# The spectral part of a ViT-block-plus-AFNO kernel: two halves of the channels against parts of 4, 2 and 2 channel blocks, the last one kept in SBUF between the inverse transforms

## The chip, the core and the metric

The kernel runs on one core of a Trainium2 chip. The metric is the time of one execution in device microseconds. Every tensor is float32.

## The reference

The input `x` is a 48 x 48 picture of tokens with 768 channels. Layer 0 is a transformer block (layer norm, attention with 12 heads and relative positions, projection, layer norm, MLP of 3072). Layer 1 mixes in the frequency domain and is the part that matters here. Cut to its core:

```python
xf = rfft2(x, axes=(1, 2), norm='ortho')          # 48 x 25 frequencies, 768 channels
xf = xf.reshape(B, H, 25, nb=8, bs=96)            # 8 blocks of 96 channels
o1r = relu(mm(xr, w1[0]) - mm(xi, w1[1]) + b1[0])
o1i = relu(mm(xi, w1[0]) + mm(xr, w1[1]) + b1[1])
o2r = softshrink(mm(o1r, w2[0]) - mm(o1i, w2[1]) + b2[0], 0.01)
o2i = softshrink(mm(o1i, w2[0]) + mm(o1r, w2[1]) + b2[1], 0.01)
y = irfft2(o2r + 1j * o2i, s=(48, 48), norm='ortho')
return y + x
```

The eight blocks never mix: each block of 96 channels can go through the whole of layer 1 alone.

## The kernel before

Layer 0 takes the span up to about 2656 us. Its last loop, the MLP, runs in three passes `p` over 768 tokens each; after each pass `rows_forward(p)` does the forward transform along the rows: for each half `k` of the channels (384 of them) and each group `g` of 384 tokens it makes four products `zp` (L1076), copies each into a tile `zt` of its own (L1080; eight buffers) and writes that to the DRAM scratch `z1[k]` (L1085).

The spectral part (L1127 on) treats the channels in two halves of four blocks. A `Unit(half, k0)` holds four of the 25 frequencies `k` (the last unit of a half only one), so a half has seven units and the whole has 14. A unit goes through four stages, each cut into four steps `i`:

- `columns(i)`: forward transform along the columns for one frequency. One matmul for each block into `fp` (L1202), then a copy to `xf`, by VectorE for even `i` and by ScalarE for odd `i` (`balanced_copy`, L77 and L75). The data `zi` comes from `z1` through `load_frequencies` (L945), two frequencies in one transfer.
- `first(i)`: the first complex layer of one block for all four frequencies, as three real matmuls (`lp`, `lp`, `l`, L1221 to L1223); then a copy on ScalarE, `pre` on VectorE (L1229), two ReLUs on ScalarE (L1234) and a negated copy on GpSimd (L1238).
- `second(i)`: the second complex layer for one frequency, eight matmuls into `mp` (L1252), then bias on VectorE (L1256), clamp on VectorE (L1260) and the difference on GpSimd (L1261).
- `back(i)`: inverse transform along the columns for one frequency, one matmul into `yp` (L1271; one PSUM buffer), copy to `y`, and for each pair of frequencies one write to the DRAM scratch `z2` (L1277).

TensorE's order is written out by hand. In round `r`, for `i` in 0 to 3, it does `back` of unit r-3, `second` of unit r-2, `first` of unit r-1 and `columns` of unit r. When all of a half's `z2` is written, the inverse transform along the rows, `rows_back(half, g)`, can begin: for each of six token groups it loads `zo` from `z2` (L1284, 600 KB, three buffers), then makes three steps of two matmuls into `rps` (L1292; two PSUM buffers, shared with `fp`), adds the residual into `yt` on VectorE (L1295; four buffers) and writes 128 rows of the output (L1296). One such step per step of a round is interleaved from round 12 on for the first half; the rest, and all of the second half's 18 steps, stand after the last round:

```python
                    if r > len(units) // 2 + 4:
                        next(first_half, None)
            for _ in first_half:
                pass
            for _ in pieces(ends[1]):
                pass
```

All transfers of this part are issued by SP (SyncE), in one queue, in an order that the build fixes. A transfer whose data or buffer isn't ready holds up those behind it.

Of the kernel before, what the change touches and what calls it, by code (L numbers as in the profile page):

```python
# [9 lines left out]
F32 = mybir.dt.float32  # L10
# [22 lines left out]
CH = C // 2  # L33
KW = HW // 2 + 1
# [10 lines left out]
def block_then_afno(  # L45
# [49 lines left out]
    z2 = [dram.tile([HW * 2 * KW, CH], F32, name=f"z2_{k}") for k in range(2)]  # L95
# [841 lines left out]
    def load_frequencies(half, k0):  # L937

        rows = z1[half].rearrange("(r k) c -> r k c", k=KW)
        tiles = []  # L940
        for k in range(k0, min(k0 + 4, KW), 2):
            n = min(2, KW - k)
            zi = turn.tile([P, C], F32, name="zi", tag="turn")
            zi = zi[: 2 * HW].rearrange("p (k c) -> p k c", c=CH)
            nc.sync.dma_start(out=zi[:, :n], in_=rows[:, k : k + n, :])  # L945
            tiles.append(zi)
        return tiles

    with ExitStack() as mlp:
# [119 lines left out]
        def rows_forward(p):  # L1069

            for k in range(2):
                for g in (2 * p, 2 * p + 1):
                    for a, parts in enumerate(((0,), (1, 2), (3, 4), (5,))):
# [6 lines left out]
                        zt = turn.tile([2 * 2 * KW, CH], F32, name="zt", bufs=8)  # L1080
# [46 lines left out]
    with ExitStack() as sp:  # L1127
        psum = sp.enter_context(tc.tile_pool(name="ps_spec", bufs=2, space=PSUM))
        cst = sp.enter_context(tc.tile_pool(name="spec_const", bufs=1))
        zin = sp.enter_context(tc.tile_pool(name="spec_in", bufs=2))  # L1130
# [25 lines left out]
        icols = view(2 * HW, 2 * HW)  # L1156
# [18 lines left out]
        NBH = NB // 2  # L1175
# [4 lines left out]
        class Unit:  # L1180
# [4 lines left out]
            def __init__(self, half, k0):  # L1185
                self.half, self.k0 = half, k0
                self.nk = min(4, KW - k0)
                self.n = self.nk * HW
                self.zz = []

            def load(self):
                self.zi = first_loads.pop(0) if first_loads else load_frequencies(self.half, self.k0)

            def columns(self, i):
# [6 lines left out]
                for b in range(NBH):  # L1201
# [4 lines left out]
                balanced_copy(i, self.xf[:, :, :, i, :], fp)  # L1206

            def first(self, i):
# [4 lines left out]
                b = NBH * self.half + i  # L1213
# [28 lines left out]
            def second(self, i):  # L1242
# [3 lines left out]
                zz = mid.tile([2 * HW, NBH, BS], F32, name="zz", bufs=10)  # L1246
                self.zz.append(zz)
                blocks_at = NBH * self.half
                mp = psum.tile([2 * HW, NBH, BS], F32, name="mp2", tag="m")
                for e in range(NBH):  # L1250
                    for t in range(2):
                        nc.tensor.matmul(  # L1252
                            mp[:, e], self.o1[:, e, i, 1 - t : 3 - t].rearrange("p t h -> p (t h)"),
                            a2[:, blocks_at + e, t], start=(t == 0), stop=(t == 1),
                        )
                nc.vector.tensor_tensor(zz, mp, d2[:, ds(blocks_at, NBH)], ALU.add)  # L1256

                flat = zz.rearrange("p n o -> p (n o)")
                cl = mid.tile([2 * HW, CH], F32, name="cl", bufs=3)
# [3 lines left out]
            def back(self, i):  # L1263
# [4 lines left out]
                if i % 2 == 0:  # L1268
                    self.y = mid.tile([2 * HW, 2, CH], F32, name="y", bufs=3)
                yp = psum.tile([2 * HW, CH], F32, name="yp", tag="y", bufs=1)  # L1270
                nc.tensor.matmul(  # L1271
                    yp, icols, zz.rearrange("p n o -> p (n o)"), start=True, stop=True
                )
                balanced_copy(i, self.y[:, i % 2, :], yp)
                if i % 2 or i == self.nk - 1:
                    n = i % 2 + 1
                    nc.sync.dma_start(  # L1277
                        out=z2_h[self.half][:, ds(self.k0 + i + 1 - n, n), :], in_=self.y[:, :n]
                    )

        def rows_back(half, g):

            zo = zin.tile([4 * KW, 4, CH], F32, name="zo", bufs=3)
            nc.sync.dma_start(  # L1284
                out=zo, in_=z2[half][ts(g, 16 * KW), :].rearrange("(a p) c -> p a c", a=4)
            )
            yield
            for i in range(3):
                yt = mid.tile([P, CH], F32, name="yt", bufs=4)
                rp = psum.tile([P, CH], F32, name="rps", tag="f")  # L1290
# [4 lines left out]
                nc.vector.tensor_tensor(yt, rp, x1[:, 3 * g + i, ts(half, CH)], ALU.add)  # L1295
                nc.sync.dma_start(out=out[ts(3 * g + i, P), ts(half, CH)], in_=yt)  # L1296
# [152 lines left out]
```

## Time and profile before

| | |
|---|---|
| median of 3 runs | 2926.68 us (2924.24 to 2931.56) |
| time of the profiled execution | 2924.9 us |
| its span | 2922.9 us |
| TensorE busy in it | 2864.6 us (98%) |
| granted TensorE clock | 0.998 |
| first spectral matmul (`fp`) | 2672.12 us |
| end of the last round's stages, only `rps` left | about 2881.3 us |
| last `yt` (start, length) | 2919.61, 0.56 us |

The span runs from the first instruction to the last; the time of the execution is 2.0 us more. All times that follow are measured from the start of the span. A float32 matmul stands in the records as two, so the counts of the profile are twice those of the code. The records of matmuls overlap; what one costs is the distance to the next.

### The profile page before, as it was taken

To read this page: it belongs to the slowest core of one execution; us is meant where nothing else is said; L and a number is where in the kernel's file an instruction comes from. 1 tells how busy PE (TensorE), PEld (TensorE's weight loads), DVE (VectorE), ACT (ScalarE), POOL (GpSimd) and SP (SyncE) were. 2 spreads that over 40 slices of the span, in tenths; PEclk is the share of its full clock that TensorE was granted. 3 is DMA by queue.
4 is the path that set the end of the run, shared out by engine and by line. 5 is a ranking of instruction groups with operands and counts; after the bars stand their busy time and mean duration, and the time that the engine had idled before them with its cause. 6 is when DMAs were issued, how large, how long until landed. Compare 5 with 4: busy or idle time off the path is not lost. (4 is left out here: it accounts for less than half of the span.)

```text
span 2922.9 us, 40961 instructions
## 1 busy us (share of the span) xinstructions
PE 2864.6 (98%) x15659; PEld 1724.2 (59%) x15659; DVE 1791.0 (61%) x2606; ACT 936.3 (32%) x1514; POOL 609.8 (21%) x564
## 2 busy tenths in 40 slices
PE   7999999999999999999999999999999999999998
PEld 4555665555555555555555555555555555556885
DVE  5243237777777777777733666674666566665564
ACT  1011126656666565665500211122011211102331
POOL 2302110000000000000043322343332323222441
PEclk9999999999999999999999999999999999999999
DMA  3423276173462716435252111212121212113235
GB/s 127 148 88 118 92 162 123 30 135 64 82 128 41 144 34 101 109 59 87 56 177 76 43 56 53 65 64 65 57 65 54 77 54 65 54 57 99 79 93 179
DMA packets 202818, 253.03 MB, mean 87 GB/s; under 512 B 21618, under 2 KB 180978, under 8 KB 201078
## 3 DMA queue, kind: packets, MB, share of 16 engines
q1 hardware_dynamic: 202614, 250.32, 33.5%
q8 instruction: 126, 2.06, 0.3%
q14 instruction: 78, 0.64, 0.1%
HBM read 136.40 MB, written 50.14 MB: 64 GB/s over the span
## 5 line engine op out<-in xcount | busy, mean ns | idle before, releaser
L635 DVE TENSOR_TENSOR acc<-acc,main 128x768 f32<-128x768 f32 x576 | 551.9, 958 | 206.4 <-ACT main L569 149.9
L569 ACT ACTIVATE main<-sp 128x768 f32<-128x768 f32 x648 | 520.8, 812 | 138.9 <-PE sp L565 132.2
L565 PE MATMUL sp<-terms,select 64*128 64x384 f32 x1296 | 413.3, 630 | 0.0
L1051 DVE TENSOR_TENSOR main<-o,main 128x384 f32<-128x384 f32 x540 | 299.4, 557 | 40.3 <-PE o L1049 2.1
L989 PE MATMUL h<-shared,w 128*128 128x384 f32 x864 | 296.7, 486 | 0.8 <-issue 0.8
L559 PE MATMUL sp<-shared 64*128 64x384 f32 x1296 | 268.0, 490 | 2.5 <-DVE o L457 2.2
L559 PE MATMUL sp<-qT,kT 64*128 64x384 f32 x1296 | 266.7, 487 | 0.2
L612 POOL TENSOR_TENSOR inverse<-inverse,rden 128x384 f32<-128x384 f32 x36 | 46.3, 1287 | 1010.7 <-DVE rden L609 918.1
L446 PE MATMUL m<-main 128*128 128x384 f32 x756 | 247.0, 488 | 6.4 <-DVE rstd L121 3.0
L989 PEld LDWEIGHTS h<-shared,w 128*128 128x128 f32 x864 | 164.4, 190 | 116.1 <-issue 2.3
L989 PE MATMUL h<-shared,w1s 128*128 128x384 f32 x648 | 226.6, 486 | 0.0
L582 PE MATMUL op<-main,shared 128*64 128x384 f32 x1296 | 221.2, 488 | 0.0
L582 PE MATMUL op<-main,v 128*64 128x384 f32 x1296 | 219.9, 488 | 0.0
L995 ACT ACTIVATE hT<-c,vec 128x384 f32<-128x384 f32 x108 | 66.4, 615 | 466.2 <-DVE c L1001 466.1
L446 PEld LDWEIGHTS m<-main 128*128 128x128 f32 x756 | 142.6, 190 | 108.3 <-issue 8.7
L1001 DVE TENSOR_TENSOR c<-h,u 128x384 f32<-128x384 f32 x108 | 60.2, 557 | 212.3 <-PE h L989 212.3
L1049 PE MATMUL o<-w,hT 128*128 128x384 f32 x432 | 175.0, 487 | 3.0 <-DVE mv L118 2.0
L1049 PE MATMUL o<-w2s,hs 128*128 128x384 f32 x432 | 174.8, 487 | 3.1 <-DVE hs L155 3.1
L565 PEld LDWEIGHTS sp<-terms,select 64*128 64x128 f32 x1296 | 125.8, 187 | 83.9 <-issue 0.5
L989 PEld LDWEIGHTS h<-shared,w1s 128*128 128x128 f32 x648 | 123.1, 190 | 85.9
L154 POOL TENSOR_TENSOR w1s<-w 128x384 f32<-128x384 f32 x36 | 36.4, 1010 | 610.9 <-PE o L1049 289.4
L559 PEld LDWEIGHTS sp<-shared 64*128 64x128 f32 x1296 | 117.9, 187 | 61.3 <-issue 23.1
(158 smaller groups left out, 3896.8 us busy)
## 6 DMA issues: line engine op xcount, KB each, us to landing
w<-in_mlp_w_dram SPq DMA_DIRECT2D x72, 768.0 KB
terms<-col_parts SPq DMA_DIRECT2D x432, 72.0 KB
terms<-row_hi SPq DMA_DIRECT2D x216, 72.0 KB
terms<-row_lo SPq DMA_DIRECT2D x216, 72.0 KB
main<-in_qkv_w_dram SPq DMA_DIRECT2D x36, 384.0 KB
z<-zt SPq DMA_DIRECT2D x48, 150.0 KB
zo<-z SPq DMA_DIRECT2D x12, 600.0 KB
x<-in_x_dram SPq DMA_DIRECT2D x18, 384.0 KB
```

Source lines behind the costliest of these rows:

```text
L446: nc.tensor.matmul(bank, a[:, c, :], b[:, c, :], start=(first and c == 0), stop=(c == 2), skip_group_check=not first,)
L559: nc.tensor.matmul(sp[:, j, :G], kT[at, ts(kt, P)], qT[at, ts(c, G)], start=True, stop=False,)
L565: nc.tensor.matmul(sp[:, j, :G], select[at, a % 2], ready[pr, c][at, a // 2, b], start=False, stop=True,)
L569: nc.scalar.activation(p, sp[:, :, :G], AF.Exp, scale=HD**-0.5)
L582: nc.tensor.matmul(op[ts(j, 64)], v[:, kt0 + i, ts(j, 64)], ps[i][:, j, :], start=(kt0 + i == 0), stop=(kt0 + i == NT - 1),)
L612: nc.gpsimd.tensor_tensor(inverse, inverse, rden, ALU.add)
L635: nc.vector.tensor_tensor(acc, made[0] if kt == 1 else acc, p, ALU.add)
L989: nc.tensor.matmul(bank[i], a[:, c, :], b[:, c, :], start=(start and c == 0), stop=(c == 2), skip_group_check=not start,)
L995: nc.scalar.activation(h[:, i, ts(k, G)], src, AF.Gelu, bias=col(V_B1 + 2 * n + i))
L1001: nc.vector.tensor_tensor(t, src, other, ALU.add)
L1049: nc.tensor.matmul(bank[k], a, b, start=start, stop=True, skip_group_check=not start)
L1051: nc.vector.tensor_tensor(dst, bank[k], dst, ALU.add)
```

## The change

The channels go through the spectral part in three parts, `PARTS = (0, 4), (4, 2), (6, 2)` (first block, number of blocks), instead of two halves of four blocks.

- There are 21 units in place of 14: seven with four blocks and 14 with two. In a unit of two blocks a step of `columns` has two matmuls, a step of `second` four, `back` has one of 192 columns instead of 384, and `first` is empty in steps 2 and 3.
- The row transforms of part 0 are interleaved in rounds 11 to 16, those of part 1 in rounds 19 to 23 (three steps in each round); the two first loads of a part are issued a round or more ahead. After the last round stand one group of part 1 and the six groups of part 2.
- Part 2 has no scratch in DRAM. `back` copies each frequency's result from PSUM to `y` as before, and then one transfer for each frequency, SBUF to SBUF (72 KB), writes it into `z_last`, a tile of 100 partitions, 24 x 192. For this the inverse matrix has a second form with its output rows sorted by pairs, so that the 96 rows of `y` go to four partitions (`k`, `k`+25, `k`+50, `k`+75), 24 runs of 192 numbers each. `rows_back` then reads `z_last` and has no load.
- To make room, `zo` has two buffers instead of three, and shares them with a tile `zt4` of four `zt` in the MLP (two of these in place of eight single ones).

```diff
-    z2 = [dram.tile([HW * 2 * KW, CH], F32, name=f"z2_{k}") for k in range(2)]
+    z2 = [
+        dram.tile([HW * 2 * KW, n * BS], F32, name=f"z2_{k}")
+        for k, (_, n) in enumerate(PARTS[:-1])
+    ]
...
-            zi = zi[: 2 * HW].rearrange("p (k c) -> p k c", c=CH)
-            nc.sync.dma_start(out=zi[:, :n], in_=rows[:, k : k + n, :])
+            zi = zi[: 2 * HW, : 2 * n * BS].rearrange("p (k c) -> p k c", k=2)
+            nc.sync.dma_start(out=zi[:, :nk], in_=rows[:, k : k + nk, ds(c, n * BS)])
...
+                    zt4 = turn.tile([P, 4, CH], F32, name="zt", bufs=2)
...
-                        zt = turn.tile([2 * 2 * KW, CH], F32, name="zt", bufs=8)
+                        zt = zt4[: 2 * 2 * KW, a]
...
+        z_last = zin.tile([4 * KW, HW // 2, PARTS[LAST][1] * BS], F32, name="z_last")
...
                 yp = psum.tile([2 * HW, CH], F32, name="yp", tag="y", bufs=1)
+                yp = yp[:, : self.nb * BS]
                 nc.tensor.matmul(
-                    yp, icols, zz.rearrange("p n o -> p (n o)"), start=True, stop=True
+                    yp, icols[:, int(self.part == LAST)], zz.rearrange("p n o -> p (n o)"),
+                    start=True, stop=True,
                 )
                 balanced_copy(i, self.y[:, i % 2, :], yp)
-                if i % 2 or i == self.nk - 1:
+                if self.part == LAST:
+                    nc.sync.dma_start(
+                        out=z_last[self.k0 + i :: KW], in_=self.y[:, i % 2, :]
+                    )
+                elif i % 2 or i == self.nk - 1:
...
-            zo = zin.tile([4 * KW, 4, CH], F32, name="zo", bufs=3)
-            nc.sync.dma_start(
-                out=zo, in_=z2[half][ts(g, 16 * KW), :].rearrange("(a p) c -> p a c", a=4)
-            )
+            if part == LAST:
+                zo = z_last[:, ts(g, 4)]
+            else:
+                zo = turn.tile([P, 4, CH], F32, name="zo", tag="zt", bufs=2)
+                zo = zo[: 4 * KW, :, : n * BS]
+                nc.sync.dma_start(
+                    out=zo, in_=z2[part][ts(g, 16 * KW), :].rearrange("(a p) c -> p a c", a=4)
+                )
...
+        def in_turn(part):
+            gens = [rows_back(part, g) for g in range(T // G)]
+            for gen in gens[:2]:
+                next(gen)
+            yield
+            for g, gen in enumerate(gens):
+                for _ in range(3):
+                    next(gen)
+                    yield
+                for later in gens[g + 2 : g + 3]:
+                    next(later)
...
-                    if r > len(units) // 2 + 4:
-                        next(first_half, None)
-            for _ in first_half:
-                pass
-            for _ in pieces(ends[1]):
-                pass
+                    for part in range(len(PARTS) - 1):
+                        begin = per * (part + 1) + 3 + part
+                        if (r, i) == (begin, 3) or (begin < r <= begin + 6 and i < 3):
+                            next(ends[part])
+            for part in ends:
+                for _ in part:
+                    pass
```

## The prediction

> **What bounds the kernel now.** I read the page first, then the windows of the spectral part, then what TensorE (PE) waits for in it, then the chain of waits.
>
> ```profile
> PE 2864.6 (98%) x15659; PEld 1724.2 (59%) x15659; DVE 1791.0 (61%) x2606; ACT 936.3 (32%) x1514; POOL 609.8 (21%) x564
> ```
>
> PE bounds the whole; the change can only win where PE stands still after 2672 us. The windows of the spectral part (busy time of PE, weight loads, VectorE, ScalarE, GpSimd, then clock, DMA share, GB/s) are its first rounds, its other rounds and what comes after the last round:
>
> ```profile
> 2672.10:2757.70 85.60, 82.16 (x713) 75.11 (x713) 50.59 (x113) 34.08 (x92) 37.71 (x44) 1.00 0.31 92
> 2757.70:2881.30 123.60, 122.20 (x973) 104.39 (x974) 72.15 (x162) 43.88 (x124) 49.81 (x62) 1.00 0.34 102
> 2881.30:2922.90 41.60, 32.40 (x97) 17.39 (x95) 13.94 (x25) 0.00 (x0) 0.00 (x0) 0.99 0.66 215
> ```
>
> The last window is the place: PE is idle for 9 us of 41.6 and DMA is twice as busy. The waits of PE from 2672 us name the transfers and GpSimd:
>
> ```profile
> PE rps L1292 <- DMA zo<-z: 5.2, 5, 1.6
> PE mp L1252 <- POOL o L1238: 3.7, 10, 0.4
> PE rps L1292 <- DVE yt L1295: 0.7, 1, 0.7
> ```
>
> The chain gives the price of each matmul group and the shape of the end:
>
> ```profile
> 2699.62 0.68 PE fp L1202 x8
> 2700.30 0.65 PE yp L1271 x2
> 2700.95 1.36 PE mp L1252 x16
> 2703.28 0.68 PE fp L1202 x8
> ...
> 2715.58 0.65 PE yp L1271 x2
> ...
> 2881.31 6.17 PE rps L1292 x20
> 2887.49 6.80 DMA zo<-z
> 2894.42 3.87 PE rps L1292 x12
> 2898.29 7.30 DMA zo<-z
> 2905.73 3.87 PE rps L1292 x12
> 2909.60 5.73 DMA zo<-z
> 2915.47 4.12 PE rps L1292 x12
> 2919.61 0.56 DVE yt L1295
> ```
>
> PE's work adds up from these: 50 steps of `columns` at 0.68, 48 of `first` at 3 x 0.33 and 8 narrow ones at 0.47, 50 of `second` at 1.36, 50 of `back` at 0.65, 36 of `rps` at 1.29: 34.0 + 47.0 + 3.8 + 68.0 + 32.5 + 46.4 = 231.7 us. From 2672.1 to 2919.6 there are 247.5 us, so 15.8 us are idle. Of these 7.5 lie after 2881.2 (38.4 us for 24 steps of 1.29 = 30.9). The rest is mostly round boundaries: a round takes 2715.58 - 2700.30 = 15.28 us where four steps of 3.66 make 14.64. The 0.64 is the wait for the last negated block:
>
> ```profile
> 2713.51 0.41 PE L1252 MATMUL mp<-shared,o 96*96 96x96 f32 x2 [0.40 <-POOL o L1238]
> ```
>
> The timeline has ten of these: rounds 2 to 7 and 9 to 12.
>
> **The work that is cut up.** A matmul costs its columns: 0.085 us a record at 96, 0.163 at 192, 0.323 at 384. Halving `yp` and `rps` changes 50 and 72 records by 0.003: +0.2 us. Bounds 0 and +2 (weight loads of 128 columns are not shown behind 192-column matmuls; the nearest, 96 behind 96, fit in 0.085). The MLP's `zt4` lets a copy wait for the transfers of the group before last, instead of the eighth before; a group takes 3.9 us, and the last 192 KB output had moved 1.4 us after its issue, so I take 0 (bounds 0 and 2).
>
> **Gain 1: no `zo` loads for the last 18 steps.** The 7.5 us go, as far as nothing new is late.
>
> **Gain 2: boundaries.** In a unit of two blocks the last `first` stands in step 1, not 3. Its chain (copy 0.32, `pre` 0.55, two ReLUs 0.80, negation 0.70, with gaps some 2.8 us) then has 3.9 us of PE work in front of its reader. Rounds 9 to 12 lose their wait: 4 x 0.64 = 2.6. Rounds 2 to 7 keep it.
>
> **Gain 3: the very end.** The last add shrinks from 0.56 to about 0.35 (the 384-column form takes 0.554, the 96-column one 0.254) and the last write is half as long: 0.4.
>
> Together 10.5 us; no more than that is there to be had.
>
> **Loss 1: one `yp` buffer.** A copy of `yp` ends about 0.8 us after its matmul at 384 columns, 0.65 at 192. Before, `first` or `second` always stood between two `yp`. Now round 8, steps 2 and 3, has only `columns` (0.34) between: two waits of 0.5, and one of 0.3 in round 16. In round 22 VectorE's fixed order puts the bias and clamp of the last unit ahead of the copy of `yp`: 0.65, and again 0.65 in front of the last `yp`. Sum 2.6; bounds 0 and 5.
>
> **Loss 2: SP's queue.** Every transfer of the part stands in one queue, now 25 SBUF writes more and the `z2` writes, outputs and loads of two parts. The queue order of the changed kernel shows three loads close to their use. The load of the last unit's `zi` stands behind the write of unit 16's last frequency, one round step before it is needed; 3.0 us of PE work against a copy, two issues of 0.3 and a 72 KB transfer: 0.2 us. The loads of part 1's groups 4 and 5 (300 KB) stand behind the `z_last` writes of round 22's first and round 23's only `back`. Counting from PE's last step of `back` in round 22, step 0: that copy ends at 1.95, its write is issued at 2.0, the load at 2.35; the lone part of a transfer starts 0.75 after its issue (last output: issued 2920.2, moving from 2921.0). With some 2.4 us for 300 KB it lands at 5.5, where PE arrives at 5.3: 0.25. Group 5's load is issued after the last `y`, at 6.3, lands at about 9.6, and PE has been waiting since 7.6: 2.0. Together 2.5. Bounds: 0, and 7 if 300 KB take as long as 600 KB did (5.7 to 7.3). Behind a waiting `rps` stands everything, since it is PE's own queue.
>
> **Loss 3: the pace of the end.** 24 steps of 192 columns alternate between two PSUM buffers: 0.66 of matmul, `yt` starts 0.27 behind, takes 0.35, and PE goes on 0.1 later: two steps in 1.38, or 0.69 instead of 0.65: 24 x 0.04 = 0.9. If `yt` stayed at 0.56 it would be 0.8 a step, 3.6 in all. `yt` has four buffers, 2.8 us around; an output lands about 1.9 us after its add if nothing stands ahead of it.
>
> **The `z_last` writes.** No row of before shows a transfer into four partitions. The nearest rows: 128 partitions alone (the last output) against 100 partitions alone (a `zo`), with the DMA share next to last:
>
> ```profile
> 2921.00:2921.50 0.50, 0.00 (x0) 0.00 (x0) 0.00 (x0) 0.00 (x0) 0.00 (x0) 1.00 0.94 356
> 2912.25:2912.90 0.65, 0.65 (x4) 0.39 (x3) 0.43 (x1) 0.00 (x0) 0.00 (x0) 1.00 0.60 201
> ```
>
> So the shape decides how many of the 16 engines work. At full share 72 KB take 0.2 us; if one engine in four works, at a sixteenth of 356/0.94 GB/s each, 0.8; if a packet of 768 bytes costs as much as one of 1536 (144 packets in about 0.6 us on 16 engines, 0.065 each) then 24 x 0.065 = 1.6. No row decides; I take the middle, 0.8. With nine writes from round 21 on that is 7 us in the 25 us until `z_last` is read, behind group 5; 1.6 would be 14 and still fit. So 0; bounds 0 and 2.
>
> The Trainium skill, "DMA: Bandwidth & Descriptors", section "Why a DMA increments its semaphore by 16 and not by 1", says that a transfer uses the largest number of engines up to 16 that divides the slowest dimension of both sides: 10 of 16 for 100 partitions, which the 0.60 bears out, and 4 for this write. By it the cost would be the 0.8 to 1.6 taken above and not 0.2; it speaks against the new write, though not enough to turn the sum.
>
> **Sum.** -10.5 + 0.2 + 2.6 + 0.2 + 2.3 + 0.9 = -4.3 us: 2924.9 - 4.3 = 2920.6 for the profiled execution. The median before is 1.8 higher than that execution, so I predict 2926.68 - 4.3 = 2922.4 us, 0.15% less. A measurement of this kernel can tell about 0.3%, or 8.8 us, from no change; so the forecast is no measurable change.
>
> **Rivals.**
> *All of the idle goes.* The loads of groups 4 and 5 come in time and the copies are faster than I reckon: -10.5, 2916.2 us. For it: losses 1 and 2 rest on gaps of tenths. Against it: group 5's load can't be issued before the last `y`. It is over 0.3% by 1.7 us only.
> *The idle moves.* The end, with no loads, runs at the pace of its 24 small outputs and their four buffers: if one takes 3.6 us around instead of 2.8, a step costs 0.9, 24 x 0.21 = 5 more than my sum: +0.7, 2927.4 us. For it: after 2887 us `yt` waited twice for an output (3.5 us). Against it: there 600 KB loads stood ahead.
> *Slower: the writes into four partitions bound the end.* They are 25, from round 17 on; until `z_last` is read PE has about 52 us of work. From 2.3 us each on the engines they share they take the lead, at 2.6 they finish 13 us late: +9, 2935.5 us. For it: their engines also carry `zo`, `zi` and outputs. Against it: 288 KB of `zi` at 3072-byte runs took 2.4 from issue to end.
>
> **How the numbers follow.** Forecast 0.52, all idle gone 0.25, idle moved 0.13, slower 0.10. Faster by over 0.3%: 0.25 and 0.04 from the forecast's better edge, 0.29; within: 0.48 + 0.13 = 0.61; slower: 0.10. The forecast's own range is 2917 to 2928 (the bounds of losses 1 to 3). The range reaches from 2914 (all idle gone, and 2 us of the median's height above the profile gone with the loads) to 2931 (idle moved and loss 2 at its upper bound); the slower rival stays outside.
>
> **What would show it.** Right: in the windows the last 25 us have PE at 95%; `zo` waits only for part 1's last groups, about 2 us; `mp` waits for GpSimd in rounds 2 to 7 only; `rps` of 192 columns 0.69 apart. Wrong: PE waiting for `z_last`'s writes, or for `zi` (`fp`), by more than 1 us; `yt` waiting for outputs; rounds of two blocks longer than 7.4 us without `rps` (then a copy or GpSimd chain has become the bound).

## The result and the profile after

The changed kernel takes 2936.24 us (median of 20 runs, 2928.46 to 2942.47), the kernel before beside it 2928.77 us (20 runs, 2922.69 to 2934.20). The ratio is 1.0028, with a 95% interval of 1.0022 to 1.0035: slower by 0.28%, just inside what the prediction called no measurable change, but 20 runs a side tell it apart from 1. The forecast was 4.3 us less, and the range ended at 2931.

Layer 0 ends some us earlier or later from run to run (the first `fp` starts at 2667.8 to 2677.1 us over all profiles here), so I compare the **spectral part**: from the start of the first `fp` to the end of the span. It took 2922.9 - 2672.1 = 250.8 us before and 2926.7 - 2667.8 = 258.9 us after: +8.1 us, against +7.5 us between the medians. The whole loss is there.

The first line of the page hardly moves, with 2864.6 us before:

```profile
PE 2865.8 (98%) x15781; PEld 1741.6 (60%) x15781; DVE 1803.0 (62%) x2700; ACT 939.7 (32%) x1538; POOL 617.6 (21%) x589
```

The windows of the spectral part (columns as in the prediction; it starts 4.3 us earlier here, so the edges are moved with it, but for the second, which lies 1.0 us further on; the last window of before is cut in two):

```profile
2667.80:2753.40 85.60, 82.16 (x713) 75.11 (x713) 50.40 (x113) 34.02 (x92) 37.69 (x44) 1.00 0.27 81
2753.40:2876.00 122.60, 118.88 (x922) 104.68 (x923) 76.72 (x212) 42.53 (x128) 46.13 (x73) 1.00 0.42 121
2876.00:2901.00 25.00, 21.95 (x175) 20.14 (x173) 14.27 (x45) 6.16 (x20) 8.02 (x14) 1.00 0.37 105
2901.00:2926.70 25.70, 20.04 (x96) 18.42 (x96) 8.59 (x24) 0.00 (x0) 0.00 (x0) 0.85 0.39 124
```

The first rounds are the same to the hundredth. The middle, which had 1.4 us of idle TensorE, now has 3.7; the end is no longer short of DMA (share 0.37 and 0.39 for 0.66), and TensorE still stands for 8.7 us in the last two windows: it is busy for 78% of the last 25.7 us, where the prediction asked for 95%. And the last clock is 0.85. What TensorE waits for in the part:

```profile
PE yp L1285 <- DVE y L78: 3.9, 6, 1.0
PE rps L1317 <- DMA zo<-z: 3.2, 2, 1.7
PE mp L1264 <- POOL o L1251: 2.5, 7, 0.4
PE fp L1213 <- DMA zi<-z: 1.1, 1, 1.1
PE yp L1285 <- ACT y L76: 1.1, 3, 0.5
```

Before, there was no wait on `yp` or `zi` at all. The five `zo` waits have become two, and GpSimd's ten have become seven: those two gains came. How the `yp` wait is made shows in round 18, step 3 (TensorE's line, then VectorE's):

```profile
2864.02 0.54 PE L1285 MATMUL yp<-zz,shared 96*96 96x192 f32 x2 [1.04 <-DVE y L78]
...
2862.68 0.35 DVE L1268 TENSOR_TENSOR zz<-mp,shared 96x192 f32<-96x192 f32 x1 [0.44 <-PE mp L1264]
2863.02 0.35 DVE L78 COPY xf<-fp 96x192 f32<-96x192 f32 x1
2863.29 0.32 DVE L1272 TENSOR_SCALAR cl<-zz 96x192 f32<-96x192 f32 x1
2863.53 0.34 DVE L78 COPY y<-yp 96x192 f32<-96x192 f32 x1
```

The matmul into `yp` of step 2 was issued at 2861.47 and its copy could have run ahead of `zz`; VectorE had stood idle for 0.44 us until 2862.68. In VectorE's program it comes behind `zz`, `xf` and `cl`. The chain of waits has SyncE's issues in it (SPq), which before it did not:

```profile
2874.97 0.35 DVE y L78
2875.34 0.64 SPq L1292
2876.04 0.46 SPq L1322
2876.60 0.64 SPq L1292
2877.34 2.70 DMA zi<-z
2880.08 0.58 PE fp L1213 x4
...
2900.89 0.64 SPq L1292
2901.63 0.63 SPq L1292
2902.36 5.09 DMA zo<-z
2907.59 16.16 PE rps L1317 x84
```

L1292 is the write to `z_last`: 0.64 us to issue, each. And the granted clock (the third column from the end) in the tail:

```profile
2902.00:2905.50 3.50, 3.50 (x11) 3.50 (x12) 0.71 (x2) 0.00 (x0) 0.00 (x0) 0.51 0.52 157
2908.80:2912.20 3.40, 3.40 (x13) 3.30 (x12) 1.09 (x4) 0.00 (x0) 0.00 (x0) 0.51 0.27 87
2912.20:2924.00 11.80, 11.53 (x67) 10.28 (x66) 6.00 (x18) 0.00 (x0) 0.00 (x0) 1.00 0.40 134
```

Twice TensorE runs at half its clock for 3.4 us, after it had waited for a `zo`: eleven and thirteen matmul records there, where the full clock has some 20 (67 in 11.8 us). About 1.7 us are lost each time. The two stretches have the same length, and the last section shows what decides whether a wait brings one.

### The profile page after: what moved, and what is told of

Same layout as the page of the kernel before. It is cut to its first block, busy times and chain, and to the rows that moved or that the text cites. A ratio compares the mean times of both kernels' runs of the same rounds, so it can differ in the third digit from the quotient of the medians.

```text
span 2926.7 us, 41582 instructions
## 1 busy us (share of the span) xinstructions
PE 2865.8 (98%) x15781; PEld 1741.6 (60%) x15781; DVE 1803.0 (62%) x2700; ACT 939.7 (32%) x1538; POOL 617.6 (21%) x589
```

## The experiments

All comparisons are with the kernel before on the same chip. The ratio is of medians over many executions. "Spectral part" is from one profiled execution of each kernel, and how much it varies between executions was not measured. In two runs the profiled execution lay far above its median (`z_last` issued by ScalarE: 2953.3 for 2944.3 us; by pairs with outputs by ScalarE: 2935.3 for 2930.6); there the ratio is the better guide. "At clock 0.50" adds up the stretches of the spectral part in which TensorE had half its clock; of what TensorE runs in them, half is lost.

| kernel | spectral part, us | at clock 0.50, us | ratio of times, 95% interval |
|---|---|---|---|
| before | 250.8 | 0 | 1 |
| changed | 258.9 | 6.8 | 1.0028 (1.0022 to 1.0035) |
| two halves of `yp` | 259.4 | 10.2 | 1.0043 (1.0028 to 1.0059) |
| early `zo` | 254.6 | 0 | 1.0017 (1.0007 to 1.0026) |
| `yp` halves, early `zo` and `zi` | 257.7 | 3.4 | 1.0028 (1.0015 to 1.0041) |
| last part by DRAM | 262.4 | 15.3 | 1.0044 (1.0028 to 1.0059) |
| two parts of four, by DRAM | 261.0 | 6.8 | 1.0042 (1.0026 to 1.0057) |
| wide `y` | 257.5 | 13.7 | 1.0023 (1.0012 to 1.0034) |
| wide `y`, early `zo` and `zi` | 256.6 | 3.4 | 1.0025 (1.0015 to 1.0034) |
| the same with `yt` halves | 250.7 | 3.4 | 0.9993 (0.9983 to 1.0003) |
| `z_last` issued by ScalarE, early loads | 274.6 | 30.7 | 1.0062 (1.0048 to 1.0076) |
| VectorE by hand | 265.1 | 6.8 | 1.0049 (1.0033 to 1.0064) |
| VectorE by hand, all buffers | 258.7 | 0 | 1.0021 (1.0013 to 1.0030) |
| `yt` halves, rows one round later | 252.2 | 3.4 | 0.9997 (0.9987 to 1.0006) |
| `yt` halves, rows two rounds later | 254.1 | 3.4 | 1.0011 (0.9998 to 1.0023) |
| one round later, loads by pairs | 250.8 | 3.4 | 0.9999 (0.9990 to 1.0009) |
| `yt` halves, last outputs by ScalarE | 250.2 | 0 | 1.0005 (0.9996 to 1.0013) |
| by pairs, last outputs by ScalarE | 256.4 | 10.2 | 1.0012 (1.0003 to 1.0020) |

### Taking the change apart

**Last part by DRAM.** The parts stay 4, 2, 2, and the 25 writes to `z_last` become 13 writes to a third `z2` and six loads.

```diff
-        for k, (_, n) in enumerate(PARTS[:-1])
+        for k, (_, n) in enumerate(PARTS)
...
-        LAST = len(PARTS) - 1
-        z_last = zin.tile(...)
+        LAST = -1
```

> Parts of 4, 2 and 2 blocks as in the changed kernel, but the last part goes through a third scratch tensor in DRAM and is read back by eight-group loads like the others; the 25 writes to `z_last` become 13 writes of pairs. Theory A: `yp` waits as they are (6.7 us); zi's 1.2 us gone or halved, as SyncE issues half as many in the last rounds; at the end the groups of the last part are read back by loads of half the width (102 packets-deep, about 150 KB) behind the last column transforms: a wait of 2 to 3 us before the first and 0.5 to 1 us before each later one, so 4 to 8 us; the spectral part takes 259 to 264 us, slower than the changed kernel by 0 to 5 us: the direct way is worth that much. Theory B (the issues and writes of `z_last` cost the time): 253 to 256 us, faster than the changed kernel.

Measured: 262.4 us, within the expectation of theory A, so with the direct way the part is 3.5 us shorter. This is a net figure, and mostly clock: without the direct way TensorE runs for some 13 us at half clock and loses 6.5 us by it, where the changed kernel loses 3.4. Of the rest, the `zo` waits are 4.9 us longer (a load of the last part has 300 KB here, not the 150 of the expectation), and the `yp` and `zi` waits are 4.6 shorter. The waits on `yp` of rounds 18 to 22 all but went (0.9 us left from round 16 on), with the same single `yp` buffer:

```profile
PE rps L1316 <- DMA zo<-z: 8.1, 4, 3.7
PE yp L1284 <- ACT y L76: 0.9, 3, 0.5
```

VectorE's program had another order here: pre, y, zz, xf, cl. So the single buffer alone does not make these waits.

**Two parts of four, by DRAM**, that is, the same with `PARTS = (0, 4), (4, 4)`: the parts of the kernel before with the row transforms, loads and two `zo` buffers of the changed one.

> Two parts of four blocks, both through DRAM, as in the kernel before; of the change there stay the row transforms in turn with loads two groups ahead, the two `zo` buffers in place of three, and the order in which the first part's row transforms stand after the later rounds. Theory A: rounds 9 to 12 lose their waits at the boundary as in the changed kernel (2.6 us less than before), round 8/9's and the halved yp waits of parts of two blocks are absent, and the end reads six groups by loads of 614 KB, two ahead: 7 to 10 us of waits there, as before or 1 to 3 us more with one buffer less; 248 to 252 us. A rival: the row order itself costs what the change cost: 255 us or more.

Measured: 261.0 us, so the rival held. Four things that are longer than before make nearly 9 of the 10.2 us. `rps` waits for `zo` 10.0 us for 5.2, since three row transforms stand between the last `back` and the first load's data where the kernel before kept six in hand (the first of these waits is 5.3 us). Behind that wait the clock is at 0.50 until 2900.16, which costs TensorE some 2.3 us. GpSimd's waits are 13 for 10, or 1.1 us more, and waits on `yp` make 0.7. The three kernels give a path: the row transforms' new order with two `zo` buffers +10.2 us, the cut into 4, 2, 2 another +1.4, the direct way -3.5; together +8.1. Each step has the clock of its profile in it, and the sizes hold in this order only.

### The `yp` waits

**Two halves of `yp`.** One PSUM tile whose two halves of 192 columns alternate.

```diff
...
+                    yp = yp_pair[0][:, ts(i % 2, self.nb * BS)]
```

> In the parts of two blocks the PSUM buffer `yp` becomes two halves of 192 columns that alternate; the part of four blocks keeps its one buffer. Theory A (each new wait has a cause of its own, and the 8.1 us that the spectral part grew, from 250.8 to 258.9 us, are their sum): the waits on `yp` of rounds 16 to 22 (0.5 + 1.2 + 1.0 + 1.0 + 2.0 = 5.7 us) go, round 8/9's 1.0 us stays, the zi and zo waits stay; the spectral part takes 253 to 255 us, the whole some 4 to 5 us less than the changed kernel. Theory B (SyncE's queue paces the last rounds: 25 issues for `z_last` at 0.64 us each, and the loads behind them): the waits on `yp` go, but TensorE then arrives earlier at zi and at the zo loads of groups 4 and 5 and waits there longer; the spectral part stays above 257 us. Theory C (the lost time is VectorE's, which is full in the rounds of two blocks): the waits move to `fp` and `mp2` of the same rounds, and 258 us stay.

Measured: 259.4 us; the `yp` waits add up to the same within 0.1 us. The step that was 1.04 us late:

```profile
2870.70 0.54 PE L1291 MATMUL yp<-zz,shared 96*96 96x192 f32 x2 [1.04 <-DVE y L78]
```

Step 3 still waits for VectorE's copy, which is step 2's, out of the other half. The edit did not give TensorE a second buffer, and so tells nothing of what one would bring. There is no second bank to give it: all eight are in use.

**Wide `y`.** Three SBUF tiles `y` hold twelve results in place of six; nothing of PSUM changes.

```diff
-                if i % 2 == 0:
+                if i % (4 if self.part == LAST else 2) == 0:
                     self.y = mid.tile([2 * HW, 2, CH], F32, name="y", bufs=3)
+                    if self.part == LAST:
+                        self.y = self.y.rearrange("p a (b c) -> p (a b) c", b=2)
...
```

> In the last part one SBUF tile `y` holds four column results of 192 in place of two, so that the same three tiles cover twelve writes to `z_last` in place of six; nothing else is changed. In the changed kernel VectorE's program places the copy out of `yp` of rounds 18 and 19 behind zz, xf and cl of the next step; with this edit it stands ahead of zz again (pre, y, zz, xf, cl). Theory A (the waits on `yp` of rounds 18 and 19 come from VectorE's order, which is arranged around `y` tiles that come free late behind the slow writes to `z_last`): 1.2 + 1.0 + 1.0 us and some of round 22's go; the spectral part falls from 258.9 to 254.5 to 256 us; zi and zo waits and the half clock in the tail stay, or TensorE arrives earlier there and waits up to 1 us more. Theory B (one PSUM buffer of `yp` is too few for steps of two blocks, whatever VectorE's order): the waits stay, 258 to 259 us.

Measured: 257.5 us, where theory A had 254.5 to 256. VectorE at the same step as above:

```profile
2865.93 0.56 DVE L1242 TENSOR_TENSOR pre<-lp,p_both 96x384 f32<-96x384 f32 x1 [0.61 <-ACT p_both L1240]
2866.40 0.34 DVE L78 COPY y<-yp 96x192 f32<-96x192 f32 x1
2866.92 0.35 DVE L1268 TENSOR_TENSOR zz<-mp,shared 96x192 f32<-96x192 f32 x1 [0.18 <-PE mp L1264]
```

The copy is ahead of `zz`, and with it all of VectorE's waits on `yp` in rounds 18 to 22 are gone, 4.5 us: theory A in its cause. Not in its sum: some 3 us of it came back at the next late load.

```profile
2903.23 3.25 PE L1321 MATMUL rps<-zo,shared 100*128 100x192 f32 x9 [3.58 <-DMA zo<-z]
```

```profile
2901.70:2908.40 6.70, 4.21 (x12) 3.70 (x12) 1.07 (x3) 0.00 (x0) 0.00 (x0) 0.50 0.50 150
2908.40:2915.20 6.80, 6.32 (x20) 6.35 (x21) 1.43 (x4) 0.00 (x0) 0.00 (x0) 0.50 0.20 63
```

TensorE came earlier to the same late load, waited 3.6 us for 1.5, and then ran at half clock for 13.7 us. The windows' clock was 1.00 again after that.

**VectorE by hand.** VectorE's order in the last part's rounds as the code is written.

```diff
...
+                if r == 2 * per:
+                    by_hand.enter_context(tc.manual_schedule(engines={mybir.EngineType.DVE}))
```

> The changed kernel, with VectorE's instructions of the last part's rounds in the order in which the kernel is written (y, zz, cl, both, pre, xf, yt step by step, as TensorE's already are) in place of the order that the scheduler finds. No buffer and no load is changed. Theory A: the waits on `yp` of rounds 18 to 22 go (3.2 and some 1.3 of 2.0 us), the waits for zi (1.2 us) and zo (3.4 us, or up to 2 us more as TensorE comes earlier) and the half clock stay: 255.5 to 257.5 us. Theory B (the copies of `y` really wait for the writes to `z_last` that read their tile): the waits on `yp` stay, 258 us or more, and the profile shows VectorE's y waiting for a DMA.

Measured: 265.1 us. VectorE's waits on `yp` went, and no `y` waited for a write to `z_last`, which is against theory B; but the written order has both operands `both` behind `cl`, and `l` waits for them fifteen times, 0.4 to 0.7 us each and 7.8 in all (shown below in the run that has everything else too). It missed the number by 8 us.

### The loads and what stands behind them

**Early `zo`.** Two groups share a `zo` buffer in part 1; a load goes three groups ahead.

```diff
+                    if g % 2 == 0:
+                        zo_pair[:] = [turn.tile([P, 4, CH], F32, name="zo", tag="zt", bufs=2)]
+                    zo = zo_pair[0].rearrange("p a c -> p (a c)")[: 4 * KW, ts(g % 2, 4 * n * BS)]
...
-            for gen in gens[:2]:
+            ahead = 2 if PARTS[part][1] == NBH else 3
...
```

> In part 1 the row transforms' groups share the two `zo` buffers two by two, and a group's load is issued three groups ahead in place of two. Nothing else changes. Theory A: the waits for zo of groups 4 and 5 (1.7 and 1.7 us) go, and with them both stretches at clock 0.50 in the tail (some 3.5 us), if it is the idle TensorE that brings the clock down; the spectral part takes 251.5 to 253 us. Theory B (SyncE's queue): the loads stand behind the same writes to `z_last`, whatever the buffer; less than 1.5 us is won. Theory D (the clock falls in the tail by itself, as nothing but short row transforms run there): the waits go and the half clock stays: 255 to 256 us, and the profile shows a granted clock of 0.50 in the last 25 us.

Measured: 254.6 us, -4.3, between the numbers of theories A and D. No wait for `zo` is left and the granted clock is 1.00 to the end, as A has it and against D. A new wait came: TensorE 1.25 us for `yt`, and VectorE 1.8 us for the output that held the buffer.

```profile
2912.80 4.40 PE L1325 MATMUL rps<-z_last,shared 100*128 100x192 f32 x24 [1.25 <-DVE yt L1329]
...
2912.39 0.36 DVE L1329 TENSOR_TENSOR yt<-rps,main 128x192 f32<-128x192 f32 x1 [1.81 <-DMA out_dram<-yt]
```

**`yp` halves, early `zo` and `zi`**: the two edits above, and the last unit's load one round earlier.

```diff
-                if r < len(units):
+                if r < len(units) - 1:
                     units[r].load()
+                if r == len(units) - 2:
+                    units[r + 1].load()
```

> The two halves of `yp`, the half buffers of `zo` three groups ahead, and the last unit's load of zi one round earlier, all together. Theory A: 5.7 (`yp`) + 1.2 (zi) + 3.4 (zo) + 3.5 (clock) = 13.8 us less at most; 12 us taken, so a spectral part of 245 to 248 us, below the 250.8 of the kernel before, and a ratio to the kernel before of 0.998 to 0.999. Theory B (SyncE's queue paces the last rounds): 3 to 6 us are won and the tail waits for zo or `z_last` take the rest; 253 us or more, ratio 1.000 or above. Theory D (half clock by itself): 249 to 251 us, ratio 0.999 to 1.000, with a granted clock of 0.50 in the tail.

Measured: 257.7 us, three more than with the early `zo` alone and on theory B's side by the number, but not by its waits: none is for `zo` or `z_last`. The wait for `zi` is gone, and VectorE's program has changed with the loads: five of the waits on `yp` in rounds 20 to 22 are new or longer (0.5, 0.9, 0.9, 0.9, 0.9 us).

**Wide `y`, early `zo` and `zi`**: the same with the wide `y` in place of the `yp` halves.

> The wide `y` tile, the half buffers of `zo` with loads three groups ahead, and the last unit's load of zi one round earlier. Theory A (order of VectorE, late zi, late zo, and the half clock as a consequence of the idle): from the 254.6 us with the early zo alone, 3.2 to 4.5 us (`yp`) and 1.2 us (zi) go, which gives 249 to 250.5 us, against 250.8 in the kernel before: a ratio of 0.999 to 1.000. Theory B (SyncE's queue paces the end: the 25 issues at 0.64 us and the outputs behind them): what is won in rounds 18 to 20 comes back as waits of `yt` for its outputs, of the first row transforms of `z_last`, or at half clock; 252 us or more.

Measured: 256.6 us, on theory B's side. From round 18 on, all waits on `yp` but 1.2 us, and those on `zi` and `zo`, are gone, and this stands in their place:

```profile
PE rps L1329 <- DVE yt L1333: 6.6, 7, 1.4
DVE yt L1333 <- DMA out_dram<-yt: 4.9, 5, 1.8
```

But the first five of the seven lie ahead of the tail, where VectorE waits for no output: there `yt` stands behind `zz`, `cl` and `pre` of later steps in its program, as `y` did.

**The same with `yt` halves.** In parts of two blocks a `yt` tile holds two results.

```diff
...
+                    if (3 * g + i) % 2 == 0:
+                        yt_pair[:] = [mid.tile([P, CH], F32, name="yt", bufs=4)]
+                    yt = yt_pair[0][:, ts((3 * g + i) % 2, n * BS)]
```

> The kernel with the wide `y` and the early zo and zi loads, and besides, in the parts of two blocks, a `yt` tile of 384 columns holds the results of two row transforms: eight half buffers in place of four. In the run without this, TensorE waited 6.6 us for `yt` in rounds 20 to 22 and the tail: VectorE's program had `yt` behind the next steps' zz and cl, and in the tail `yt` waited for outputs up to 1.8 us. With it VectorE's program has yt ahead of zz in rounds 20 and 21. Theory A (VectorE's order, arranged around buffers that are taken to come free late, sets where TensorE waits): 4 to 6 us of these go, the spectral part takes 250.5 to 252.5 us. Theory B (SyncE's queue is too slow for the last rounds and the end): the waits for `yt` move on to the tail, 255 us or more.

Measured: 250.7 us, within theory A's 250.5 to 252.5, and 0.9993 in time: the kernel before is reached. 5.9 us came from a buffer, with the same work on every engine.

**VectorE by hand, all buffers**, is this kernel with VectorE's order as written, and nothing else.

> VectorE's order by hand in the last part's rounds, with the wide `y`, the half buffers of `zo` and `yt`, and the early zo and zi loads. Theory A: of the waits only round 8/9's 1.2 us, the last rounds' yp (0.7) and some outputs' stay; the spectral part takes 247.5 to 250.5 us, against 250.8 in the kernel before, and the ratio to it is 0.999 to 1.000. Theory B (SyncE's queue): 253 us or more, with waits of `yt` for outputs or of TensorE for `z_last` in the tail.

Measured: 258.7 us. Between the two only VectorE's order differs, and it moves the spectral part by 8.0 us, as much as the whole change did, and the medians by 6.2. The half clock is no part of it: this run has none, the other 3.4 us.

```profile
PE l L1236 <- DVE both L1231: 6.1, 12, 0.7
```

(The line covers the rounds from 2840 us on; three more of these waits, 1.8 us, lie ahead of it.) Both theories missed: A by its number, and B, whose number of 253 or more was met, by the waits that it named: they are for `l`, and only one, of 1.2 us, stands before `z_last`.

**`z_last` issued by ScalarE**, with the early loads.

```diff
-                    nc.sync.dma_start(
+                    nc.scalar.dma_start(
                         out=z_last[self.k0 + i :: KW], in_=self.y[:, i % 2, :]
```

> As the changed kernel with the early zo and zi loads, and the 25 writes to `z_last` are issued by ScalarE in place of SyncE; `y` stays as it was. It tells what the writes cost SyncE's queue from what their transfers cost. VectorE's order has the copies of `y` ahead of zz here too. Theory A: ScalarE loses some 0.6 us for each of 25 issues, beside its copies of a few us a round; its activation of `o` and copies of p_both come later, and `mp2` waits for `o` 0.3 to 0.6 us in rounds 17 to 21; the outputs no longer wait behind `z_last` on SyncE, so `yt` waits for nothing: 249 to 252 us. Theory B (SyncE's queue is what paces the end): 246 to 248 us, below the kernel before by 3 us or more.

Measured: 274.6 us, far off both. Half of the writes take a `y` that VectorE copies. ScalarE's queue stands until that copy is done, and its own work behind it:

```profile
PE yp L1285 <- ACT y L76: 9.3, 6, 2.4
```

A window there:

```profile
2910.00:2920.00 10.00, 10.00 (x47) 9.74 (x46) 3.08 (x11) 1.15 (x5) 1.66 (x3) 0.50 0.15 47
```

Five stretches at 0.50, 30.7 us together, lie between 2869.7 and 2927.8 us, each behind such a wait (1.9 to 2.4 us), with a clock of 1.00 between them. The issue costs 0.64 us here too, so the price goes with the write, not with SyncE; whether its shape or its target in SBUF makes it was not taken apart. What the writes cost SyncE's queue was not learned from this.

### What ends last, once the waits are gone

With the `yt` halves one wait is left in the tail, before the first row transform of `z_last`. The profile puts it down to an output; the issue of the last two writes to `z_last` ends 3.9 us ahead of its end (timeline, SyncE's line and TensorE's):

```profile
2900.71 1.37 SPq L1296 DMA_DIRECT2D z_last<-y  x2
...
2905.95 14.09 PE L1336 MATMUL rps<-z_last,shared 100*128 100x192 f32 x72 [1.67 <-DMA out_dram<-yt]
```

**Rows one and two rounds later** put nine and twelve row transforms of part 1 in between, for six.

```diff
-                        begin = per * (part + 1) + 3 + part
+                        begin = per * (part + 1) + 3 + 2 * part
```

> The kernel with the wide `y`, the half buffers of `zo` and `yt` and the early loads (spectral part 250.7 us), and besides, part 1's row transforms start one round later, so that nine of them in place of six stand between the last column transform and the first row transform of `z_last`. In the run without this, TensorE stood 1.7 us before that first row transform, which the profile puts down to an output; the last write to `z_last` had left SyncE 3.9 us earlier. Behind the wait the granted clock was 0.50 for some 3.5 us (1.7 us lost). Theory A (the wait is for the last write to `z_last` to land, and the half clock follows from the idle): both go, 247 to 248.5 us, a ratio of 0.998 to 0.999 to the kernel before. Theory B (the wait is for outputs in SyncE's queue, or the clock falls at this place anyway): 249.5 us or more, and a granted clock of 0.50 in the last 20 us.

> The same with part 1's row transforms two rounds later: twelve of them behind the last column transforms, none in rounds 19 and 20. Theory A: what was one wait is covered already with nine, so nothing more is won: within 0.7 us of the run with one round later. If VectorE's yt copies of rounds 19 and 20 held up something there, 0.5 to 1 us less. Theory B (outputs in SyncE's queue pace the end): the three more row transforms come in the stretch that their outputs already fill, so 1 to 2 us more than with one round later.

Measured: 252.2 and 254.1 us. The first row transform of `z_last` waits for nothing in either, as theory A has it; but group 5's load is now late instead (3.0 us, and 3.4), and half clock follows in both. Theory A's numbers missed. Theory B's came (249.5 or more, and one to two more for the second), but by this load and not by the outputs that B names.

**One round later, loads by pairs**: groups 0 to 3 at the start, 4 and 5 behind group 1.

> The kernel with part 1's row transforms one round later (spectral part 252.2 us), and its zo loads issued by pairs: groups 0 to 3 at the start, groups 4 and 5 behind group 1. With one round later alone, the first row transform of `z_last` waited for nothing, but group 5's waited 3.0 us for its load, issued 5 us before, behind the last writes to `z_last`; the clock was 0.50 for 3.4 us behind it (1.7 us). Theory A (a late load is what is left, the half clock its consequence): both go, 247 to 248.5 us, with no granted clock under 0.9 ahead of the end, and a ratio of 0.998 to 0.999 to the kernel before. Theory B (something always ends late in the tail, as the writes to `z_last`, the outputs and the loads share SyncE's queue and the transfers): a wait of 1.5 us or more stands elsewhere, 250 us or more.

Measured: 250.8 us. The load is in time; now `yt` waits 2.2 us for an output and the first `rps` of `z_last` 1.25 us, and half clock follows. Theory B's number.

**Last outputs by ScalarE**, on the kernel with `yt` halves and on the one by pairs.

```diff
-                nc.sync.dma_start(out=out[ts(3 * g + i, P), at], in_=yt)
+                (nc.scalar if at_end else nc.sync).dma_start(out=out[ts(3 * g + i, P), at], in_=yt)
```

> The kernel with the wide `y`, the half buffers of `zo` and `yt` and the early loads (spectral part 250.7 us), and besides, the outputs of the row transforms that stand after the last round are issued by ScalarE, which has nothing else to do there, in place of SyncE. In the run without this TensorE stood 1.7 us before the first row transform of `z_last`, and the clock was 0.50 for some 3.5 us behind it. Theory A (that wait is for the last writes to `z_last` to land, which the outputs in the same queue hold up little): the wait stays within 0.7 us of 1.7, and so does the half clock: 250 to 251 us. Theory B (outputs in SyncE's queue make it late): the wait falls under 0.5 us and the half clock goes: 247 to 248.5 us, a ratio of 0.998 to 0.999.

> The same edit on the kernel whose row transforms come one round later with loads by pairs (250.8 us). There `yt` waited 2.2 us for an output ahead of the first row transform of `z_last`, which so came 1.3 us late, with a half clock behind it. Theory A (the transfers are slow, the queue does not matter): within 1 us of 250.8. Theory B (outputs queue on SyncE behind the writes to `z_last`): the 1.3 + 1.7 us go, 247 to 248.5 us, a ratio of 0.998 to 0.999, below both the kernel before and the changed one.

Measured: 250.2 and 256.4 us. In the first theory A's number came (250 to 251), and the wait did not go, though the outputs had left SyncE's queue. It even grew, to more than A allows, and the half clock that A keeps went. It grew because the last two writes to `z_last` left later, behind an output of the rounds that waited for its `yt`:

```profile
2903.85 1.37 SPq L1296 DMA_DIRECT2D z_last<-y  x2
...
2908.54 12.47 PE L1337 MATMUL rps<-z_last,shared 100*128 100x192 f32 x72 [2.79 <-issue]
```

Its windows, with the clock at 1.00 in spite of that wait:

```profile
2904.00:2908.00 4.00, 1.75 (x11) 1.36 (x9) 1.07 (x3) 0.00 (x0) 0.00 (x0) 1.00 0.47 147
2908.00:2912.00 4.00, 3.46 (x20) 3.24 (x21) 1.43 (x4) 0.00 (x0) 0.00 (x0) 1.00 0.40 129
```

The last issue ends at 2905.22, TensorE goes on 3.3 us later. SyncE's queue holds nothing but these two writes then (the outputs of 2903.42 and before are out, the next is issued at 2908.89). It moves its last ten packets between 2907.5 and 2908.0 and none from there to 2908.6, so the wait is for these writes to land, as theory A has it. In the second, `yt` waits twice for outputs, 3.0 and 2.7 us, more than without the edit, and both numbers missed. Here the last `z_last` writes left SyncE at 2910.1 to 2912.6, behind two outputs of the rounds, some 5.7 us later than without the edit, and TensorE's second wait ends 2.3 us after them. Why the second of those outputs was issued so late is not shown. None of the sixteen kernels beats the one before; five can't be told from it.

## Why the prediction was wrong

**Gain 1 (no `zo` loads for the last 18 steps): right.** No such load is in the tail, and the last 18 row transforms wait for nothing. By the gaps between TensorE's starts it brought 6.8 us.

**Gain 2 (boundaries): right, less.** Three of four waits went, one of 0.4 stayed: 1.7 us for 2.6.

**Loss 1 (one `yp` buffer): the step that failed first.** The places in round 8, 16 and 22 were right, and cost what was said or a little more. Rounds 18 and 19 were missed: 1.2 + 1.0 + 1.0 us. In all 6.7 us for 2.6, above the bound of 5. The term looked for two `yp` with too little work between, and used VectorE's order in round 22 only. In round 18 there is work enough between; the copy itself stands behind `zz`, `xf` and `cl`. Wide `y` and VectorE by hand both change VectorE's order and leave the single `yp` as it is, and in both these waits are gone, so VectorE's order is shown as their cause. Alone, wide `y` won only 1.4 us of the part, since other waits and the clock took the rest. That the scheduler places `y` and `yt` late because it takes their buffers to come free late, behind the writes to `z_last`, fits all of these runs, but what the scheduler assumes was not seen.

**Loss 2 (SP's queue): the right loads, too short.** `zi` 1.2 us for 0.2, `zo` 3.4 for 2.25. An issue was taken at 0.30 us, and the write to `z_last` takes 0.64; the load of group 5 took 5.1 us from its issue to its landing for the 3.2 of the estimate (0.75 + 2.4), though within the bound of 7. The wait for `zi`, by over 1 us, is one of the signs of being wrong that the prediction named.

**A term that was not there: the clock.** Two stretches at half, some 3.5 us in all. The kernel before has the same kind of waits in its tail (five, up to 1.6 us) at a clock of 1.00, and I took the clock for given. By the last section part of this is luck: it depends on where a wait falls. With these terms (4.1 + 0.9 + 1.0 + 1.2 + 3.5 us, and 0.7 less from gain 1) the sum goes from -4.3 to +7.1 of the 8.1 measured; the remaining 1.0 us is not placed.

**Loss 3 (pace of the end): right.** From 2913.5 to 2923.8 us a step takes 0.69. **Gain 3 (the very end): right.** The last add takes 0.36 us for 0.56, and what follows it 2.54 for 2.73: 0.4.

**The `z_last` writes: the price was near.** One of them moves alone, from 2859.25 to 2860.30 us: 1.05 us for the 0.8 taken, at a DMA share of 0.25 (next to last column), a quarter of the 16 engines:

```profile
2859.50:2860.00 0.50, 0.50 (x8) 0.50 (x7) 0.50 (x2) 0.31 (x1) 0.19 (x1) 1.00 0.25 80
```

**The range** was too narrow at its slow end: the upper bounds of losses 1 to 3, all taken together, give 2932, not 2928. But 2936 lies above that too, so this is not where it failed.

**The rivals.** The slower one came nearest in time, but not by its mechanism: in the changed kernel TensorE never waits for a write to `z_last`. (One of ScalarE's copies into `y` is put down to such a write, 1.8 us at 2899.45, with 0.54 us of waiting on `yp` behind it; with the wide `y` the same 0.5 us are there without it.) The mechanism is real, though, one layer down: of the three kernels that came to 250 or 251 us, two end on that wait (1.7 and 2.8 us). "The idle moves" is what the experiments show at every turn, but by VectorE's order and late loads, not by the outputs' four buffers, which came into play only with the early `zo`.

## What to carry to other kernels

A change that cuts the work finer rearranges every engine whose order is not fixed by hand: price it by the new program order of each, from buffers to who stands behind whom, not only by durations. Ask for each step moved to the end how much work is left to cover the transfer that it waits for; with three in hand where there had been six, the wait for the first load grew to 5.3 us. And remove waits in the order in which they come in time: several that went here only brought TensorE earlier to the next late transfer, and of the edits tried it took three together (wide `y`, early loads, `yt` halves) to return the 8 us.

## What was not expected of the hardware

A write from 96 partitions into four, 24 runs of 768 bytes each, takes 0.64 us to issue, on SyncE and on ScalarE alike, where the write of `y` to DRAM takes 0.30 to 0.39.

The granted clock of TensorE falls to 0.50 in the tail and stays so for 3.4 us, or for whole multiples of it when another wait comes. A wait went before every fall of the spectral part, from 1.0 us (`yp` halves with the early loads) over 1.25 (loads by pairs), 1.5 and 1.7 (changed) to 3.6 (wide `y`) and 5.3 (two parts of four). But not every wait was followed by one: five of up to 1.6 us before, 1.25 with the early `zo` and 2.8 with the outputs by ScalarE were not. So the length of the wait does not decide it.

What does is in the traces: a grid. In each profile the stretches at 0.50 begin whole multiples of 3.413 us apart (before: at 426.90, 1549.89, 1648.87 and 1962.90 us, which are 329, 29 and 92 of them), so the clock changes on a grid of 3.41 us. Layer 0 has a test of it that is the same in all 18 kernels: at about 424 to 431 us TensorE waits 2.17 us for a tile `o`. In nine profiles the clock fell there, in nine it did not. Where it fell, the wait lay wholly or nearly so in one interval of the grid; where it did not, a grid line cut it in two, with at least 0.4 us on either side. There is no exception, and as the code is the same, the kernel does not choose where the grid lies. Two of the eighteen, one of either kind, in intervals of the grid (columns as before: PE first, the clock third from the end), before and changed:

```profile
423.49:426.90 3.41, 1.24 (x20) 0.94 (x17) 1.47 (x3) 0.86 (x2) 0.00 (x0) 1.00 0.58 217
426.90:430.31 3.41, 3.41 (x16) 2.46 (x14) 0.33 (x1) 2.85 (x4) 0.00 (x0) 0.50 0.62 120
```

```profile
423.97:427.38 3.41, 1.68 (x12) 1.31 (x14) 1.46 (x3) 0.98 (x3) 0.00 (x0) 1.00 0.18 62
427.38:430.79 3.41, 2.82 (x24) 1.74 (x22) 0.96 (x1) 3.40 (x5) 0.00 (x0) 1.00 0.68 112
```

Before, TensorE was busy for 1.24 of the 3.41 us, 36%, and the next interval has half clock; in the changed kernel the same wait left it 1.68 us, 49%, in one interval and 2.82 in the next, and the clock stayed. Over all 18 profiles, of the intervals at full clock, each of the 59 with TensorE busy for less than 42% was followed by half clock, 16 of 63 between 42 and 58%, and none above 58%. So a wait is priced by how much of it falls into one interval. In a single profile that is chance, and a difference of some 2 us between two spectral parts of the table can be this chance alone.

The Trainium skill, "TensorE: Matmul & The Clock Gate", section "Part 1: The HAM clock gate (the "warmup" mystery)", says that the clock is halved after an idle window of some 3.4 us and that these windows run freely, without regard to the kernel. The grid of 3.41 us agrees with that; a fall after an interval in which TensorE was busy for 36% of the time, or after a wait of 1.0 to 1.7 us, does not agree with a whole idle window.
